# A two-layer graph attention kernel: an overflow test without bounds, the query by one VectorE operation, more buffers, and another order of setup and end

## The chip, the core and the metric

The kernel runs on one core of a Trainium2 chip. The time is device microseconds of one launch, the median of several runs. All runs quoted of one kernel, taken together, agree within about 0.3%. The profile is one further execution, recorded with the hardware profiler.

## The reference, cut to what matters

32 images of 512 nodes by 512 features, float32, one 512 x 512 adjacency matrix of zeros and ones for all. Two layers, each on a normalised input and added to it:

```python
# layer 0: attention of 8 heads, 64 wide
h = relu(layernorm(x))
q, k, v = h @ Wq + bq, h @ Wk + bk, h @ Wv + bv          # split into heads
s = q @ k.T / sqrt(64) + (1 - adj) * -1e9
x = x + (softmax(s) @ v) @ Wo + bo
# layer 1: graph attention
h = relu(layernorm(x))
g = h @ W;  s1 = g @ a1;  s2 = g @ a2
e = leaky_relu(s1[i] + s2[j], 0.2) * adj
x = x + elu(softmax(e) @ g + beta * g)
```

The kernel takes the softmaxes without subtracting a row maximum. That is right as long as no exponential overflows, so it has to find out at the end whether one could have; if so, a slow general path does everything again. With these inputs that path never runs.

## The kernel before: the parts concerned

The work is a software pipeline. In one iteration TensorE does the scores and the attention of image b, the projections of image b+1, the output projection and the logits of layer 1 of image b-1, and the final stage of layer 1 of image b-2. TensorE's order is written by hand; that of the other engines is made by the framework from the program and from when it thinks an operand is ready.

The query leaves PSUM through ScalarE and is scaled on GpSimd. Both projections are read a second time for a bound on the scores:

```python
def proj_q(b, hT, f, qT):                       # [...] the matmuls into p
    qf = wtile([P, N], f"qf_{b}_{f}", "qf", 1)
    nc.scalar.activation(qf, p, AF.Identity, bias=bq_c[:, f : f + 1])
    q = wtile([P, N], f"qT_{b}_{f}", "qT", 6)
    nc.gpsimd.tensor_tensor(q, qf, edge8, op=ALU.mult)
    bound(b, f, qm[:, f, :], p, bq_c[:, f : f + 1])

def bound(b, f, m, p, bias):                    # [...] first image of a group of 8
    r = wtile([P, N], f"ab_{b}_{f}", "ab", 1, BF16)
    nc.scalar.activation(r, p, AF.Abs, bias=bias)
    nc.vector.tensor_tensor(m, m, r, op=ALU.max)
```

The exponentials `e` of a pair of heads are added up on GpSimd into one buffer `es`, which TensorE then multiplies by ones to have the denominators `pd`:

```python
    if k == 1:
        st["es"][j] = wtile([P, 2, N], f"es_{b}_{j}", "es", 1)      # one buffer
    if k:
        one, es = (st["e"][j][0] if k == 1 else st["es"][j]), st["es"][j]
        for s in range(2):
            nc.gpsimd.tensor_tensor(es[:, s, :], one[:, s, :], e[:, s, :], op=ALU.add)
# attend():
        nc.tensor.matmul(pd[...], ones[:, :HD], st["es"][j][:, s, :], start=True, stop=True)
    nc.vector.reciprocal(rd, pd)
    nc.gpsimd.tensor_tensor(o, o, rd, op=ALU.mult)
```

The final stage ends on GpSimd with the addition of the residual `x1`, whose buffer the load of a later residual waits for. That load is followed on GpSimd by an addition of a constant row, and in the same queue stand the small powers that give each row its 1/sqrt(variance):

```python
def final(b, t, st):                            # [...] matmuls into p
    nc.scalar.activation(y, p, AF.Exp, scale=r)
    nc.vector.tensor_scalar(y, y, 1.0, -1.0, op0=ALU.min, op1=ALU.add)      # the clamp
    nc.vector.scalar_tensor_tensor(y, p, r, y, op0=ALU.mult, op1=ALU.max)
    nc.gpsimd.tensor_tensor(y, y, st["x1"][t], op=ALU.add)
    nc.sync.dma_start(out[b, ts(t, P), :], y)
def residual(b, st):                            # for each t
    nc.sync.dma_start(r, x[b, ts(t, P), :])
    nc.gpsimd.tensor_tensor(r, r, c_row, op=ALU.add)
def stats(...):                                 # [...] mean and variance on VectorE
    nc.gpsimd.tensor_tensor(rstd, rstd, mhalf[:, 0:1], op=ALU.pow)
```

## Time and profile before

| | before |
|---|---|
| median of the first 3 runs | 4221.7 us (4221.6 to 4225.3) |
| TensorE busy | 94% |
| setup, until the pipeline's first transposition | 104.2 us |
| pipeline, until the last value projection | 3896.4 us |
| tail | 220.5 us |

The same three stretches, as the trace has them (columns: from:to, us, then busy us of TensorE, its weight loads, VectorE, ScalarE and GpSimd with counts, the granted clock, the DMA share and GB/s):

```profile
0.00:104.20 104.20, 62.04 (x142) 28.84 (x143) 31.91 (x72) 19.64 (x31) 21.30 (x32) 0.93 0.30 101
104.20:4000.60 3896.40, 3754.54 (x11051) 1507.40 (x11049) 2306.43 (x3131) 1344.72 (x1865) 1836.78 (x1553) 0.99 0.08 24
4000.60:4221.10 220.50, 166.96 (x442) 66.68 (x442) 97.78 (x161) 46.66 (x64) 73.09 (x62) 0.87 0.07 23
```

What TensorE waited for before (who waited, for which engine's writing, total us, times, the longest):

```profile
PE ps L268 <- DVE e L272: 51.2, 27, 3.3
PE pk L226 <- DVE at L351: 45.3, 25, 3.9
PE pq L215 <- ACT ab L238: 18.6, 20, 2.3
...
PE pe L367 <- POOL as L361: 17.4, 2, 8.8
PE pbs L116 <- DVE dgs L111: 14.9, 2, 7.6
```

The first three recur in most iterations (20 to 27 of 31) and are the three holes that the prediction shows in one of them. The last two come twice, at the end, and are the holes of the tail. One caution in reading them: in about every other iteration some of TensorE's matmuls ran slowly (from 632 to 641 us the granted clock was 0.81), and its waits were then shorter by what it lost. The iteration that starts at 411.1 us has 5.3 us of waits. In the next one the eight score matmuls take 2.88 us and not 2.26, those of the query projection 4.45 and not 3.70, 1.4 us lost together though the wait before them was only 1.9 us, and the waits come to 3.9 us. Both iterations took 127.82 us.

### The profile page before, as it was taken

What the parts mean: (1) busy time and instruction counts of PE and PEld (TensorE: products, weight loads), DVE (VectorE), ACT (ScalarE), POOL (GpSimd) and SP (SyncE); (2) the same over time, 40 slices, a digit from 0 to 9 for tenths busy, and PEclk for the clock granted to TensorE, in tenths of its full rate; (3) what the DMA queues carried; (4) which work ended last, traced back from release to release, by engine and by line L of the source; (5) the groups of instructions that cost most, each with busy time, mean ns of one, the idle gap of its engine ahead of it and who ended that gap; (6) DMA issues with size and microseconds to landing.
All of it is one profiled execution on the core that took longest, in us unless ns stands there. A gap on an engine that the chain in (4) does not pass through costs nothing.

```text
span 4221.1 us, 32429 instructions
## 1 busy us (share of the span) xinstructions
PE 3983.5 (94%) x11632; PEld 1602.9 (38%) x11632; DVE 2436.1 (58%) x3364; ACT 1411.0 (33%) x1960; POOL 1931.2 (46%) x1647
## 2 busy tenths in 40 slices
PE   5999999999999999999999999999999999999986
PEld 2333333333343333333333333333433333333332
DVE  3556655556655566555666555666555665556663
ACT  1433333333333333333333333333333333333321
POOL 2444544445444445444545444454444454444451
PEclk9999999999999999999999999999999999999988
DMA  2000000000110000100000100001100001000000
GB/s 100 20 10 30 20 30 25 26 20 20 30 30 25 20 25 20 30 28 22 20 30 20 30 25 25 20 21 30 30 25 20 25 20 30 29 21 11 20 20 28
DMA packets 59000, 109.91 MB, mean 26 GB/s; under 512 B 6416, under 2 KB 6416, under 8 KB 58832
## 3 DMA queue, kind: packets, MB, share of 16 engines
q1 hardware_dynamic: 55824, 101.74, 7.9%
q10 hardware_dynamic: 2640, 5.24, 0.4%
q8 instruction: 93, 1.52, 0.2%
q0 software_dynamic: 368, 0.79, 0.1%
q14 instruction: 75, 0.61, 0.0%
HBM read 74.19 MB, written 33.55 MB: 26 GB/s over the span
## 4 chain that ended last, share of the span: by engine, by line
PE 60%; DVE 20%; POOL 7%; ACT 6%; DMA 5%; issue 1%; SPq 0%; ACTq 0%; POOLq 0%; DVEq 0%
PE pg L380 11%; PE pv L258 11%; PE po L290 8%; PE py L390 8%; PE pk L226 6%; PE ps L268 6%; DMA x<-in_x_dram 4%; PE pq L215 4%; DVE e L272 3%; DVE scr L337 3%; PE pw L319 3%; DVE rd L303 2%; POOL rs L184 2%; DVE x L200 2%; ACT e L275 2%; PE pd L297 2%
## 5 line engine op out<-in xcount | busy, mean ns | idle before, releaser
L282 POOL TENSOR_TENSOR es<-es,e 128x512 f32<-128x512 f32 x512 | 671.6, 1340 | 476.2 <-ACT e L275 476.2
L272 DVE TENSOR_TENSOR e<-ps,nmT 128x1024 f32<-128x1024 f32 x512 | 608.0, 1215 | 476.6 <-PE ps L268 476.6
L275 ACT ACTIVATE e<-e 128x1024 f32<-128x1024 f32 x512 | 541.1, 1057 | 747.8 <-DVE e L272 724.6
L282 POOL TENSOR_TENSOR es<-e,e 128x512 f32<-128x512 f32 x256 | 323.8, 1286 | 700.3 <-PE pd L297 696.3
L303 DVE RECIPROCAL rd<-pd 128x512 f32<-128x512 f32 x128 | 429.4, 3355 | 365.2 <-PE pd L297 365.2
L268 PE MATMUL ps<-qT,kT 64*128 64x512 f32 x2048 | 527.3, 631 | 52.6 <-DVE e L272 51.2
L226 PE MATMUL pk<-hT,wk 128*128 128x512 f32 x1024 | 482.7, 616 | 55.7 <-DVE at L351 45.3
L215 PE MATMUL pq<-hT,wq 128*128 128x512 f32 x1024 | 476.9, 609 | 22.0 <-ACT ab L238 18.6
L390 PE MATMUL py<-w,gT 128*128 128x512 f32 x1024 | 472.1, 605 | 0.8 <-ACT ab L238 0.8
L290 PE MATMUL po<-e,v 128*64 128x512 f32 x2048 | 469.9, 601 | 0.0
L319 PE MATMUL pw<-wo,oT 128*128 128x512 f32 x1024 | 463.5, 596 | 4.0 <-DVE y L398 3.6
L380 PE MATMUL pg<-at,hn 128*128 128x512 f32 x1024 | 458.6, 601 | 0.8 <-DVE at L375 0.8
L258 PE MATMUL pv<-wv,hT 128*128 128x512 f32 x1024 | 456.3, 598 | 0.0
L313 POOL TENSOR_TENSOR x<-x,c_row 128x512 f32<-128x512 f32 x128 | 163.0, 1275 | 346.7 <-DMA x<-in_x_dram 346.7
L226 PEld LDWEIGHTS pk<-hT,wk 128*128 128x128 f32 x1024 | 192.1, 194 | 336.7 <-issue 224.4
L268 PEld LDWEIGHTS ps<-qT,kT 64*128 64x128 f32 x2048 | 176.4, 188 | 357.9 <-issue 211.9
L215 PEld LDWEIGHTS pq<-hT,wq 128*128 128x128 f32 x1024 | 193.7, 195 | 299.4 <-issue 218.3
L390 PEld LDWEIGHTS py<-w,gT 128*128 128x128 f32 x1024 | 185.8, 190 | 279.8 <-issue 251.0
L380 PEld LDWEIGHTS pg<-at,hn 128*128 128x128 f32 x1024 | 190.3, 191 | 265.7 <-issue 233.2
L319 PEld LDWEIGHTS pw<-wo,oT 128*128 128x128 f32 x1024 | 194.3, 191 | 253.9 <-issue 242.8
L399 POOL TENSOR_TENSOR y<-y,x 128x512 f32<-128x512 f32 x128 | 162.2, 1267 | 272.7 <-DVE y L398 270.5
L258 PEld LDWEIGHTS pv<-wv,hT 128*128 128x128 f32 x1024 | 189.6, 190 | 243.6 <-issue 215.2
(113 smaller groups left out, 3655.6 us busy)
## 6 DMA issues: line engine op xcount, KB each, us to landing
x<-in_x_dram SPq DMA_DIRECT2D x256, 256.0 KB, 2.9
out_dram<-y SPq DMA_DIRECT2D x128, 256.0 KB, 3.2
wq<-in_L_gnn_Wq_dram ACTq DMA_DIRECT2D x1, 1024.0 KB, 12.7
adj_sb<-in_adj_dram SPq DMA_DIRECT2D x1, 1024.0 KB, 9.6
wk<-in_L_gnn_Wk_dram ACTq DMA_DIRECT2D x1, 1024.0 KB, 16.1
wv<-in_L_gnn_Wv_dram ACTq DMA_DIRECT2D x1, 1024.0 KB, 18.2
wo<-in_L_gnn_Wo_dram ACTq DMA_DIRECT2D x1, 1024.0 KB, 20.4
w<-in_L_gnn_W_dram ACTq DMA_DIRECT2D x1, 1024.0 KB, 17.8
```

The source lines that it names most:

```text
L215: nc.tensor.matmul(p, wq[:, c, ts(f, P)], hT[c], start=c == 0, stop=c == C - 1)
L226: nc.tensor.matmul(p, wk[:, c, ts(f, P)], hT[c], start=c == 0, stop=c == C - 1)
L258: nc.tensor.matmul(p, hT[c][:, ts(t, P)], wv[:, c, :], start=c == 0, stop=c == C - 1)
L268: nc.tensor.matmul(p[:, s, :], st["kT"][j][rows, ts(k, P)], st["qT"][j][rows, :], start=True, stop=True)
L272: nc.vector.tensor_tensor(e, p, nmT[:, k, :].unsqueeze(1).to_broadcast([P, 2, N]), op=ALU.add)
L275: nc.scalar.activation(e, e, AF.Exp)
L282: nc.gpsimd.tensor_tensor(es[:, s, :], one[:, s, :], e[:, s, :], op=ALU.add)
L290: nc.tensor.matmul(po[s * HD : (s + 1) * HD, :], v[k][:, (2 * j + s) * HD : (2 * j + s + 1) * HD], e[k][:, s, :], start=k == 0, stop=k == ...
L303: nc.vector.reciprocal(rd, pd)
L319: nc.tensor.matmul(p, st["oT"][c][:, ts(t, P)], wo[:, c, :], start=c == 0, stop=c == C - 1)
L380: nc.tensor.matmul(p, st["hn"][k][:, ts(c, P)], st["at"][k], start=k == 0, stop=k == T - 1)
L390: nc.tensor.matmul(p, st["gT"][c][:, ts(t, P)], w1[:, c, :], start=c == 0, stop=c == C - 1)
```

## The change

The intent is to take work off the chain between the engines. No bounds are kept: an overflow is found from what it leaves. The values are scaled by 2^60 so that an overflow reaches the means and variances as a value that isn't finite, and the sums of the reciprocals and the totals of layer 1 are checked against 2^60. The query becomes one VectorE operation that reads PSUM. Some buffers become more numerous, the first projections come ahead of the constants, and the end has another order. The core of the diff:

```diff
 def proj_q(b, hT, f, qT):
-        qf = wtile([P, N], f"qf_{b}_{f}", "qf", 1)
-        nc.scalar.activation(qf, p, AF.Identity, bias=bq_c[:, f : f + 1])
         q = wtile([P, N], f"qT_{b}_{f}", "qT", 6)
-        nc.gpsimd.tensor_tensor(q, qf, edge8, op=ALU.mult)
-        bound(b, f, qm[:, f, :], p, bq_c[:, f : f + 1])
+        nc.vector.scalar_tensor_tensor(
+            q, p, bq_c[:, f : f + 1], edge8, op0=ALU.add, op1=ALU.mult
+        )
 def proj_k(b, hT, f, kT):
-        bound(b, f, km[:, f, :], p, bk_c[:, f : f + 1])
 # [...] bound, bound_rows, bound_group removed; in logits():
-        nc.scalar.activation(sa, s12.rearrange("p g t -> p (g t)"), AF.Abs)
-        nc.vector.tensor_tensor(smax, smax, sa, op=ALU.max)
 # [...] value projection: scaled by VS = 2^60; residual: p * 1/VS + x1 in one operation
-            st["es"][j] = wtile([P, 2, N], f"es_{b}_{j}", "es", 1)
+            st["es"][j] = wtile([P, 2, N], f"es_{b}_{j}", "es", 2)
 # [...] likewise rd 1 -> 2, x1 5 -> 6, y 2 -> 3; in attend():
+        nc.scalar.activation(junk, rd, AF.Copy, accum_out=rsum[:, b, j : j + 1])
 # in diagonal():
+        nc.vector.scalar_tensor_tensor(fin, st["mv"], 0.0, fin, op0=ALU.mult, op1=ALU.add)
+        nc.vector.tensor_tensor(dmax[:, 0, :], dmax[:, 0, :], pd[:, :, 0], op=ALU.max)
+        nc.vector.tensor_tensor(dmax[:, 1, :], dmax[:, 1, :], rd, op=ALU.max)
 # the last stages; the verdict (judge) becomes a part of the one before the last
+        if b == B:
+            order = G + Y[:2] + W + Y[2:3] + lg + Y[3:] + D + [judge]
 # setup: first image and Wq first, constants between the projections
+        load_w(wq, Wq)
         new_state(0)
+        load_adj()
+        # [...] the other weights
         norm0(0, states[0]["x"])
         # [...] transpositions
+        edges()
+        first = list(front_groups(0))
+        # first[:4]: the first two query and key projections
+        # [...] load and normalise image 1
+        masks()
+        # first[4:]: the other projections
+        row_constants()
```

More of the change, by code (lines that the diff above doesn't have):

```diff
@@ L23 @@
 BIG = 3.0e38
-LIM0 = 30.0
-LIM1 = 40.0
-GROUP = 8
+VS = 2.0 ** 60
+RMAX = 2.0 ** 60
 def bcast_rows(ap, n):
@@ L72, in ctile, with load_w @@
         return const.tile(shape, dt, name=name, tag=name)
-    def load_w(ap, name):
-        w = ctile([P, C, D], name)
+    wq, wk, wv, wo, w1 = (ctile([P, C, D], n) for n in ("wq", "wk", "wv", "wo", "w1"))
+    def load_w(w, ap):
         nc.scalar.dma_start(w, ap.rearrange("(c p) f -> p c f", p=P))
-        return w
-    wq, wk, wv = load_w(Wq, "wq"), load_w(Wk, "wk"), load_w(Wv, "wv")
-    wo, w1 = load_w(Wo, "wo"), load_w(W, "w1")
     bq_c, bk_c, bv_c = ctile([P, C], "bq_c"), ctile([P, C], "bk_c"), ctile([P, C], "bv_c")
@@ L100 @@
     c_row = ctile([P, D], "c_row")
-    qm, km = ctile([P, C, N], "qm", BF16), ctile([P, C, N], "km", BF16)
-    bmax = ctile([P, N], "bmax")
-    smax = ctile([P, 2 * T], "smax")
+    fin = ctile([P, T, 2], "fin")
+    dmax = ctile([P, 2, T], "dmax")
+    rsum = ctile([P, B, NP], "rsum")
     bad = ctile([P, T], "bad")
-    kv = ctile([P, C, 32], "kv", BF16)
     flag = ctile([1, 1], "flag", I32)
@@ L117, in row_bcast, with wtile, load_adj, edges @@
         return p
-    with tc.tile_pool(name="setup", bufs=1) as work, tc.tile_pool(
-        name="setup_psum", bufs=2, space=bass.MemoryType.PSUM
-    ) as psum:
-        adj_sb = work.tile([P, T, N], F32, name="adj_sb", tag="adj_sb")
-        nc.sync.dma_start(adj_sb, adj.rearrange("(t p) k -> p t k", p=P))
-        deg = work.tile([P, T], F32, name="deg", tag="deg")
-        nc.vector.tensor_reduce(deg, adj_sb, axis=AX.X, op=ALU.max)
-        e0 = work.tile([P, T], F32, name="e0", tag="e0")
-        nc.vector.tensor_scalar(e0, deg, 0.0, 1.0, op0=ALU.is_equal, op1=ALU.mult)
-        sq = work.tile([P, T, N], F32, name="sq", tag="sq")
-        nc.vector.scalar_tensor_tensor(sq, adj_sb, -1.0, adj_sb, op0=ALU.add, op1=ALU.mult)
-        nc.vector.tensor_reduce(bad, sq, axis=AX.X, op=ALU.max, apply_absolute_value=True)
+    nc.vector.memset(fin, 0.0)
+    nc.vector.memset(dmax, 0.0)
+    fast = ExitStack()
+    work = fast.enter_context(tc.tile_pool(name="work", bufs=2))
+    psum = fast.enter_context(tc.tile_pool(name="psum", bufs=2, space=bass.MemoryType.PSUM))
+    def wtile(shape, name, tag, bufs, dt=F32):
+        return work.tile(shape, dt, name=name, tag=tag, bufs=bufs)
+    adj_sb = []
+    def load_adj():
+        for t in range(T):
+            r = wtile([P, N], f"adj_{t}", "at", 4)
+            nc.sync.dma_start(r, adj[ts(t, P), :])
+            adj_sb.append(r)
+    def edges():
+        e0 = wtile([P, T], "e0", "e0", 1)
+        for t in range(T):
+            nc.vector.tensor_reduce(e0[:, t : t + 1], adj_sb[t], axis=AX.X, op=ALU.max)
+        nc.vector.tensor_scalar(e0, e0, 0.0, 1.0, op0=ALU.is_equal, op1=ALU.mult)
         pe0 = row_bcast(psum, work, e0, "e0")
-        e0_r = work.tile([P, N], F32, name="e0_r", tag="e0_r")
-        nc.scalar.copy(e0_r, pe0)
-        nc.vector.tensor_scalar(edge8, e0_r, -(HD ** -0.5), HD ** -0.5, op0=ALU.mult, op1=ALU.add)
+        nc.vector.tensor_scalar(edge8, pe0, -(HD ** -0.5), HD ** -0.5, op0=ALU.mult, op1=ALU.add)
+    def masks():
         for k in range(T):
@@ L140, with row_constants @@
             for t in range(T):
-                nc.tensor.transpose(p[:, ts(t, P)], adj_sb[:, t, ts(k, P)], ident)
+                nc.tensor.transpose(p[:, ts(t, P)], adj_sb[t][:, ts(k, P)], ident)
             nc.scalar.copy(adjT[:, k, :], p)
-            m = work.tile([P, N], F32, name=f"m_{k}", tag="m", bufs=2)
-            nc.vector.tensor_tensor(m, p, e0_r, op=ALU.max)
+            m = wtile([P, N], f"m_{k}", "y", 3)
+            nc.vector.tensor_scalar(m, edge8, -(HD ** 0.5), 1.0, op0=ALU.mult, op1=ALU.add)
+            nc.vector.tensor_tensor(m, p, m, op=ALU.max)
             nc.vector.tensor_scalar(nmT[:, k, :], m, -NEG, NEG, op0=ALU.mult, op1=ALU.add)
-        wa = work.tile([P, 2, C], F32, name="wa", tag="wa")
+        for t in range(T):
+            sq = wtile([P, N], f"sq_{t}", "y", 3)
+            nc.vector.scalar_tensor_tensor(sq, adj_sb[t], -1.0, adj_sb[t], op0=ALU.add, op1=ALU.mult)
+            nc.vector.tensor_reduce(
+                bad[:, t : t + 1], sq, axis=AX.X, op=ALU.max, apply_absolute_value=True
+            )
+    def row_constants():
+        nc.gpsimd.dma_start(c_row, bcast_rows(bo, D))
+        p = psum.tile([P, D], F32, name="pc", tag="mm")
+        for c in range(C):
+            r = wtile([P, P], f"bvr_{c}", "y", 3)
+            nc.vector.tensor_copy(r, bv_c[:, c : c + 1].to_broadcast([P, P]))
+            nc.tensor.matmul(p, r, wo[:, c, :], start=c == 0, stop=c == C - 1)
+        nc.vector.tensor_add(c_row, c_row, p)
+        wa = wtile([P, 2, C], "wa", "wa", 1)
         for g in range(2):
-            ar = work.tile([P, D], F32, name=f"a_{g}", tag="ar", bufs=2)
+            ar = wtile([P, D], f"a_{g}", "x1", 6)
             nc.gpsimd.dma_start(ar, bass.AP(tensor=a.tensor, offset=a.offset + g * D, ap=[[0, P], [1, D]]))
             for c in range(C):
-                scr = work.tile([P, D], F32, name=f"scr_{g}_{c}", tag="scr", bufs=2)
+                scr = wtile([P, D], f"scr_{g}_{c}", "y", 3)
                 nc.vector.tensor_tensor_reduce(
@@ L160 @@
             nc.scalar.copy(dst, p)
-        nc.gpsimd.dma_start(c_row, bcast_rows(bo, D))
-        p = psum.tile([P, D], F32, name="pc", tag="mm")
-        for c in range(C):
-            r = work.tile([P, P], F32, name=f"bvr_{c}", tag="bvr", bufs=2)
-            nc.vector.tensor_copy(r, bv_c[:, c : c + 1].to_broadcast([P, P]))
-            nc.tensor.matmul(p, r, wo[:, c, :], start=c == 0, stop=c == C - 1)
-        nc.vector.tensor_add(c_row, c_row, p)
-        nc.vector.memset(bmax, 0.0)
-        nc.vector.memset(smax, 0.0)
-        nc.vector.memset(kv, 0.0)
-    fast = ExitStack()
-    work = fast.enter_context(tc.tile_pool(name="work", bufs=2))
-    psum = fast.enter_context(tc.tile_pool(name="psum", bufs=2, space=bass.MemoryType.PSUM))
-    def wtile(shape, name, tag, bufs, dt=F32):
-        return work.tile(shape, dt, name=name, tag=tag, bufs=bufs)
     def stats(src, t, u, mv, rstd):
@@ L215, in proj_q @@
             nc.tensor.matmul(p, wq[:, c, ts(f, P)], hT[c], start=c == 0, stop=c == C - 1)
-        qf = wtile([P, N], f"qf_{b}_{f}", "qf", 1)
-        nc.scalar.activation(qf, p, AF.Identity, bias=bq_c[:, f : f + 1])
         q = wtile([P, N], f"qT_{b}_{f}", "qT", 6)
-        nc.gpsimd.tensor_tensor(q, qf, edge8, op=ALU.mult)
-        bound(b, f, qm[:, f, :], p, bq_c[:, f : f + 1])
+        nc.vector.scalar_tensor_tensor(
+            q, p, bq_c[:, f : f + 1], edge8, op0=ALU.add, op1=ALU.mult
+        )
         qT.append(q)
@@ L228, in proj_k @@
         nc.scalar.activation(k, p, AF.Identity, bias=bk_c[:, f : f + 1])
-        bound(b, f, km[:, f, :], p, bk_c[:, f : f + 1])
         kT.append(k)
-    def bound(b, f, m, p, bias):
-        if b % GROUP == 0:
-            nc.scalar.activation(m, p, AF.Abs, bias=bias)
-        else:
-            r = wtile([P, N], f"ab_{b}_{f}", "ab", 1, BF16)
-            nc.scalar.activation(r, p, AF.Abs, bias=bias)
-            nc.vector.tensor_tensor(m, m, r, op=ALU.max)
-    def bound_rows(b):
-        kx = wtile([P, C], f"kx_{b}", "kx", 1)
-        nc.vector.tensor_reduce(kx, km, axis=AX.X, op=ALU.max)
-        nc.vector.tensor_copy(kv[:HD, :, 0:1], kx[:HD].unsqueeze(2))
-        nc.vector.tensor_copy(kv[HD:, :, 1:2], kx[HD:].unsqueeze(2))
-    def bound_group(b):
-        p = psum.tile([P, N], F32, name=f"pbd_{b}", tag="mm")
-        for f in range(C):
-            nc.tensor.matmul(p[ts(f, 32), :], kv[:, f, :], qm[:, f, :], start=True, stop=True)
-        nc.vector.tensor_tensor(bmax, bmax, p, op=ALU.max)
     def proj_v(b, hT, t, v):
@@ L259, in proj_v @@
         s = wtile([P, D], f"v_{b}_{t}", "v", 8)
-        nc.scalar.copy(s, p)
+        nc.scalar.mul(s, p, VS)
         v.append(s)
@@ L301, in attend @@
         nc.scalar.copy(o, po)
-        rd = wtile([P, N], f"rd_{b}_{j}", "rd", 1)
+        rd = wtile([P, N], f"rd_{b}_{j}", "rd", 2)
         nc.vector.reciprocal(rd, pd)
+        junk = wtile([P, N], f"rj_{b}_{j}", "rj", 1)
+        nc.scalar.activation(junk, rd, AF.Copy, accum_out=rsum[:, b, j : j + 1])
         nc.gpsimd.tensor_tensor(o, o, rd, op=ALU.mult)
@@ L310, in residual @@
         for t in range(T):
-            r = wtile([P, D], f"x1_{b}_{t}", "x1", 5)
+            r = wtile([P, D], f"x1_{b}_{t}", "x1", 6)
             nc.sync.dma_start(r, x[b, ts(t, P), :])
@@ L322, in out_proj @@
         x1 = st["x1"][t]
-        nc.vector.tensor_tensor(x1, p, x1, op=ALU.add)
-        mv = wtile([P, 2], f"mv1_{b}_{t}", "mv1", 4)
+        nc.vector.scalar_tensor_tensor(x1, p, 1.0 / VS, x1, op0=ALU.mult, op1=ALU.add)
+        if t == 0:
+            st["mv"] = wtile([P, T, 2], f"mv1_{b}", "mv1", 2)
+        mv = st["mv"][:, t, :]
         rstd = wtile([P, 1], f"rs1_{b}_{t}", "rs1", 4)
@@ L335, in out_proj @@
         for g, r in ((0, wa1_r), (1, wa2_r)):
-            scr = wtile([P, D], f"scr_{b}_{t}_{g}", "y", 2)
+            scr = wtile([P, D], f"scr_{b}_{t}_{g}", "y", 3)
             nc.vector.tensor_tensor_reduce(
@@ L344, in logits @@
         s12 = st["s12"]
-        sa = wtile([P, 2 * T], f"sa_{b}", "sa", 2)
-        nc.scalar.activation(sa, s12.rearrange("p g t -> p (g t)"), AF.Abs)
-        nc.vector.tensor_tensor(smax, smax, sa, op=ALU.max)
         p = row_bcast(psum, work, s12[:, 0, :], f"s1_{b}")
@@ L394, in final @@
         r = st["rd1"][:, t : t + 1]
-        y = wtile([P, D], f"y_{b}_{t}", "y", 2)
+        y = wtile([P, D], f"y_{b}_{t}", "y", 3)
         nc.scalar.activation(y, p, AF.Exp, scale=r)
@@ L438, in dense @@
         D = of(prev, lambda n, i: diagonal(n, s), 1)
-        whole = nxt is not None and (nxt % GROUP == GROUP - 1 or nxt == B - 1)
-        K = [(lambda: bound_rows(nxt)) if whole else None]
-        Q = [(lambda: bound_group(nxt)) if whole else None]
-        order = (
-            G + [Y[0], F[0], Y[1], F[1], W[0], Y[2], W[1], F[2], W[2], Y[3], W[3], F[3], F[4]]
-            + L + [F[5]] + lg + [F[6], F[7]] + K + [V[0], V[1]] + D + Q + [V[2], V[3]]
-        )
+        if b == B:
+            order = G + Y[:2] + W + Y[2:3] + lg + Y[3:] + D + [judge]
+        else:
+            order = (
+                G + [Y[0], F[0], Y[1], F[1], W[0], Y[2], W[1], F[2], W[2], Y[3], W[3], F[3], F[4]]
+                + L + [F[5]] + lg + [F[6], F[7]] + V[:2] + D + V[2:]
+            )
         return [g for g in order if g is not None]
@@ L462, in attention, with judge @@
         return units
+    def judge():
+        ok = wtile([P, T, 6], "ok", "ok", 1)
+        nc.vector.tensor_scalar(ok[:, :, 0:2], fin, 0.0, 1.0, op0=ALU.is_equal, op1=ALU.mult)
+        nc.vector.tensor_scalar(
+            ok[:, :, 2:4], dmax.rearrange("p g t -> p t g"), RMAX, 1.0, op0=ALU.is_le, op1=ALU.mult
+        )
+        nc.vector.tensor_scalar(ok[:, :, 4], bad, 0.0, 1.0, op0=ALU.is_equal, op1=ALU.mult)
+        rm = wtile([P, NP], "rm", "rm", 1)
+        nc.vector.tensor_reduce(rm, rsum.rearrange("p b j -> p j b"), axis=AX.X, op=ALU.max)
+        nc.vector.tensor_scalar(ok[:, :, 5], rm, RMAX, 1.0, op0=ALU.is_le, op1=ALU.mult)
+        okm = wtile([P, 1], "okm", "okm", 1)
+        nc.vector.tensor_reduce(okm, ok, axis=AX.XY, op=ALU.min)
+        p = psum.tile([1, 1], F32, name="pok", tag="mm")
+        nc.tensor.matmul(p, okm, ones[:, 0:1], start=True, stop=True)
+        nc.vector.tensor_scalar(flag, p, P - 0.5, 1.0, op0=ALU.is_lt, op1=ALU.mult)
     with tc.manual_schedule(engines=PE_ONLY):
+        load_w(wq, Wq)
         new_state(0)
+        load_adj()
+        for w, ap in ((wk, Wk), (wv, Wv), (wo, Wo), (w1, W)):
+            load_w(w, ap)
         norm0(0, states[0]["x"])
@@ L468 @@
             turn(0, states[0]["x"], states[0]["hT"], c)
+        edges()
+        first = list(front_groups(0))
+        for g in first[:4]:
+            g()
         if B > 1:
@@ L471 @@
             norm0(1, states[1]["x"])
-        for g in front_groups(0):
+        masks()
+        for g in first[4:]:
             g()
+        row_constants()
         for b in range(B + 2):
@@ L490 @@
     fast.close()
-    with tc.tile_pool(name="judge", bufs=1) as work, tc.tile_pool(
-        name="judge_psum", bufs=1, space=bass.MemoryType.PSUM
-    ) as psum:
-        m = work.tile([P, 4], F32, name="m", tag="m")
-        nc.vector.tensor_reduce(m[:, 0:1], bmax, axis=AX.X, op=ALU.max)
-        nc.vector.tensor_reduce(
-            m[:, 1:3], smax.rearrange("p (g t) -> p g t", g=2), axis=AX.X, op=ALU.max
-        )
-        nc.vector.tensor_reduce(m[:, 3:4], bad, axis=AX.X, op=ALU.max)
-        mT = psum.tile([4, P], F32, name="mT", tag="mT")
-        nc.tensor.transpose(mT, m, ident)
-        r = work.tile([4, 1], F32, name="r", tag="r")
-        nc.vector.tensor_reduce(r, mT, axis=AX.X, op=ALU.max)
-        rT = psum.tile([1, 4], F32, name="rT", tag="rT")
-        nc.tensor.transpose(rT, r, ident[:4, :4])
-        q = work.tile([1, 4], F32, name="q", tag="q")
-        nc.vector.tensor_copy(q, rT)
-        nc.vector.tensor_scalar(q[:, 0:1], q[:, 0:1], LIM0 / HD ** -0.5, 1.0, op0=ALU.is_gt, op1=ALU.mult)
-        nc.vector.tensor_add(q[:, 1:2], q[:, 1:2], q[:, 2:3])
-        nc.vector.tensor_scalar(q[:, 1:2], q[:, 1:2], LIM1, 1.0, op0=ALU.is_gt, op1=ALU.mult)
-        nc.vector.tensor_scalar(q[:, 3:4], q[:, 3:4], 0.0, 1.0, op0=ALU.is_gt, op1=ALU.mult)
-        nc.vector.tensor_add(q[:, 0:1], q[:, 0:1], q[:, 1:2])
-        nc.vector.tensor_add(q[:, 0:1], q[:, 0:1], q[:, 3:4])
-        nc.vector.tensor_copy(flag, q[:, 0:1])
-    again = nc.values_load(flag[0:1, 0:1], min_val=0, max_val=3,
-                           skip_runtime_bounds_check_because="a sum of three comparisons")
+    again = nc.values_load(flag[0:1, 0:1], min_val=0, max_val=1,
+                           skip_runtime_bounds_check_because="a comparison")
     with tc.If(again > 0):
```

## The prediction

> **What bounds the kernel now.** I read in this order: the busy table, the chain that ended last, a table by stage, one iteration in order of time, and the groups of the operations that the diff touches.
>
> ```profile
> PE 3983.5 (94%) x11632; PEld 1602.9 (38%) x11632; DVE 2436.1 (58%) x3364; ACT 1411.0 (33%) x1960; POOL 1931.2 (46%) x1647
> ...
> PE 60%; DVE 20%; POOL 7%; ACT 6%; DMA 5%; issue 1%; SPq 0%; ACTq 0%; POOLq 0%; DVEq 0%
> ```
>
> TensorE is busy 94% of the span, so everything that can be won lies in its 237 us without work and in the time it ran at half clock. Yet the chain lies on TensorE for only 60%: in part of each iteration it runs through VectorE, GpSimd, ScalarE and a DMA. By stage (columns: us, busy us of PE, PEld, DVE, ACT, POOL with counts, granted clock, DMA share, GB/s):
>
> ```profile
> 0.00:52.40 52.40, 14.88 (x30) 6.92 (x30) 23.01 (x50) 5.38 (x8) 6.04 (x17) 0.98 0.49 165
> 52.40:104.20 51.80, 47.16 (x112) 21.92 (x113) 8.89 (x23) 14.26 (x23) 15.26 (x16) 0.88 0.11 37
> 283.10:3870.80 3587.70, 3457.66 (x10150) 1390.26 (x10149) 2124.14 (x2900) 1229.16 (x1708) 1684.35 (x1429) 0.99 0.08 25
> ...
> 4101.50:4176.70 75.20, 54.35 (x127) 22.70 (x126) 29.20 (x65) 11.60 (x18) 15.98 (x15) 0.84 0.08 25
> 4176.70:4221.10 44.40, 30.34 (x66) 13.05 (x66) 7.55 (x23) 5.09 (x8) 5.05 (x4) 0.85 0.07 25
> ```
>
> Row 1 is the setup: TensorE does 15 us of work in 52. Row 3 is 28 iterations of 128.1 us each, with (3587.7 - 3457.7)/28 = 4.6 us idle each; the clock of 0.99 costs about another 1 us. So an iteration could be at best some 122.5 us. Rows 4 and 5 are the tail, with 21 and 14 us idle.
>
> Where the 4.6 us are lost, in an ordinary iteration (start, length, engine, line, operation; in brackets the idle time before it and who ended it):
>
> ```profile
> 1525.96 1.26 POOL L219 TENSOR_TENSOR qT<-qf,edge 128x512 f32<-128x512 f32 x1
> 1526.04 1.48 DVE L200 TENSOR_SCALAR x<-x,mv,rs 128x512 f32<-128x512 f32 x1 [0.66 <-POOL rs L184]
> ...
> 1529.03 2.26 PE L268 MATMUL ps<-qT,kT 64*128 64x512 f32 x8 [1.97 <-DVE e L272]
> 1530.03 0.73 DVE L351 SCALAR_TENSOR_TENSOR at<-pbs,s,adjT 128x512 f32<-128x512 f32 x1
> ...
> 1531.67 0.68 ACT L238 ACTIVATE ab<-pk,bk_c 128x512 bf16<-128x512 f32 x1
> 1532.39 0.60 DVE L239 TENSOR_TENSOR km<-km,ab 128x512 bf16<-128x512 bf16 x1 [1.62 <-ACT ab L238]
> 1532.40 3.70 PE L215 MATMUL pq<-hT,wq 128*128 128x512 f32 x8 [1.11 <-ACT ab L238]
> ...
> 1537.89 3.70 PE L226 MATMUL pk<-hT,wk 128*128 128x512 f32 x8 [1.79 <-DVE at L351]
> ```
>
> Three TensorE waits (1.97, 1.11 and 1.79 us), all around the logits of layer 1. The second is directly the score bound (ScalarE's second read of the key projection). The third is a PSUM buffer that the four logit operations free late, because VectorE stood 1.62 us waiting for that same bound and then did it. The chain of this iteration leaves TensorE at 1487.8 and returns at 1537.9: for 50 us it is a dependency chain over the small engines.
>
> **What the Trainium skill says.** "TensorE: Matmul & The Clock Gate", Part 1: the clock halves after an idle window of about 3.4 us and comes back after a busy one. The trace agrees: after a wait of 3.25 us at 3970 us the eight matmuls of one projection take 6.65 us, where they take 3.60 elsewhere; so long waits cost about double, and short ones are often free of this. "SBUF — State Buffer", Who interferes with whom: GpSimd shares a port pair with VectorE, and a VectorE operation in a two-port mode or with two SBUF inputs waits for it. The trace agrees: the normalisation above takes 1.48 us beside the q product on GpSimd, and 0.546 in the median. "PSUM — Partial Sum Buffer", The four PSUM rules, states that GpSimd cannot read PSUM; that fits the old route of q, ScalarE to SBUF and then GpSimd. "Perfetto Trace Analysis", Identifying Performance Opportunities: a bubble that repeats can mean too few buffers; here it is the two-buffer PSUM tag of the projections.
>
> **The change part by part.** Groups concerned:
>
> ```profile
> L219 POOL TENSOR_TENSOR qT<-qf,edge 128x512 f32<-128x512 f32 x128 | 166.1, 1297 | 37.5 <-ACT qf L217 37.5
> L239 DVE TENSOR_TENSOR qm<-qm,ab 128x512 bf16<-128x512 bf16 x112 | 87.1, 778 | 121.1 <-ACT ab L238 121.1
> L239 DVE TENSOR_TENSOR km<-km,ab 128x512 bf16<-128x512 bf16 x112 | 57.4, 513 | 143.9 <-ACT ab L238 143.9
> L398 DVE SCALAR_TENSOR_TENSOR y<-py,rd,y 128x512 f32<-128x512 f32 x128 | 96.1, 751 | 4.5
> ```
>
> Engine totals first. ScalarE loses q's eviction (86 us), the absolute values (152 + 22) and the small one of the logits (7), and gains 128 sums of the reciprocals, like the 630 ns exponential of L355, perhaps 0.75 with its accumulator: +96. Net about -170. GpSimd loses 166. VectorE loses 145 for the maxima and 18 for the rest of the bounds; it gains q as one operation on PSUM and one SBUF input, which the L398 row prices at 0.75 us (x128 = +96), the scale in the residual add (0.75 for 0.69, +8), and three small operations per image (about +16). Net -43. TensorE loses 1.6 us. So in totals almost nothing is taken off the bounding engine; the gain must come from waits.
>
> Setup, on the path. The first projection starts at 61.4 us. In the new order the x tiles and Wq are first in their queues: Wq landed 12.7 us after its issue even as it was, the x tiles will land some 4 to 9 us in, and from the issue of x to the first projection took 15.3 us (46.1 to 61.4), of which about 4 were GpSimd stuck on residual adds. With the edge column (adjacency, four reductions, one broadcast matmul) ahead of it I put the first projection at about 18 us, 43 earlier. TensorE then has to do what it did before: transposes of the mask (2 us, plus about 3 of waits on their evictions), row constants (two broadcasts and the bias product, 5.5 us, plus about 2 of waits). 43 - 13 = **30 us**.
>
> Iterations, on the path, following the 50 us chain. (a) At 1530.8 VectorE can go on with the logits at once: the wait of 1.62 and the maximum of 0.60 go, 2.2 us. (b) Just before, the q maximum (0.33) and the port wait of the normalisation (1.48 - 0.55) go, and one q operation of 0.75 comes: 0.5 us. (c) At 1499.4 the chain runs ScalarE q, absolute value, maximum (0.58 + 0.58 + 0.50); one q operation of 0.75 takes their place, about 0.7 us net as the two dot products before it stay. Sum 3.4 of the 5.6 us of idle and slow clock. The chain is not the only limit and the new sums and small maxima take something back; I count 80%, **2.7 us** x 29 iterations = **78 us**.
>
> Buffers: a second row-sum buffer removes GpSimd's waits for the denominators' matmul (696 us, but GpSimd isn't the bound), and a sixth residual buffer starts a load one final stage sooner; twice in the chain GpSimd stands on that load with the rstd behind it. I count both as help for the 80%, not extra.
>
> Tail. In the next-to-last stage TensorE waits 7.32 us for the logits' broadcast and 8.78 for the row sums. Y2 and Y3, 3.43 us each, are moved into these two holes: 7 us. The verdict's serial steps from 4212.0 to 4215.3, behind the last store, go before the last stage: about 4 us with the waits. The wait of 3.60 us for a final stage's buffer may also go: 2. Together **13 us**.
>
> Sum 30 + 78 + 13 = 121; 4221.7 - 121 = about 4100 us, 2.9% faster.
>
> **Rivals.** (1) VectorE takes the place: q's PSUM buffer is now freed by an engine whose queue holds reciprocals of 3.36 us and pairs of score additions of 2.34. With two buffers, an eviction may come one group (3.4 us) late without harm, and VectorE stood idle near three of the four q's; against that, the second and third q fall in the stretch where VectorE is nearly full. If each costs 1 us, the iterations win only 1 us: 4221.7 - 30 - 29 - 13 = 4150. (2) ScalarE stands behind the reciprocal: the new sum waits in its in-order queue for a 3.36 us operation; if that is late, evictions and exponentials behind it are late, and TensorE waits. The gap between the end of the denominators and the next eviction is about one group, so the cost should be tenths; if it is 1 us per head pair, that is 4 per iteration and the gain of the iterations is gone: about 4180. (3) The chain collapses altogether, with the residual loads no longer in it: TensorE is left with 0.4 us per iteration, 5.2 x 29 = 150 won, 4030. (4) Work in totals decides and waits only move: then only setup and tail count, 4180.
>
> **Range and chances.** The setup and tail are nearly certain (35 to 50 us, 1% together), so slower is very unlikely. The line of 2% is 84 us, that is, 41 us from the iterations, 1.4 us each; (a) alone would give that. Predicted 4100, 8 times in 10 between 4055 and 4155; faster by over 2% 0.77, within 2% 0.21, slower 0.02.
>
> **What would show it.** First projection near 18 us and first scores near 76 (now 107). The wait before the second query projection gone, that before the last key projection under 0.6 us, the one before the scores still 1 to 2 us; iterations near 125.4. VectorE near 2390 us, ScalarE 1240, GpSimd 1765. Wrong if TensorE waits for the q operation (rival 1), if ScalarE's idle time is ended by the reciprocal with TensorE behind it (2), or if setup is bound by VectorE or by the weights' landing.

## The result, and the profile after

| | before | after |
|---|---|---|
| median | 4221.66 us (4212.39 to 4225.29, 4 runs) | 4091.32 us (4089.47 to 4092.31, 4 runs) |
| setup | 104.2 us | 92.3 us |
| pipeline | 3896.4 us | 3790.4 us |
| tail | 220.5 us | 206.6 us |

The ratio is 0.9694, with a 95% interval of 0.9677 to 0.9711: 3.1% faster. A ratio here is the mean time of one kernel's fast runs over that of the other's of the same rounds, so it is not quite the ratio of the medians quoted. Of the 131.8 us that the two traces differ, 11.9 lie in the setup, 106.0 in the pipeline (31 iterations, 3.4 us each) and 13.9 in the tail.

The busy table of after, and its chain of work that ended last:

```profile
PE 3950.5 (97%) x11616; PEld 1590.1 (39%) x11616; DVE 2409.2 (59%) x3323; ACT 1254.4 (31%) x1799; POOL 1839.0 (45%) x1519
...
issue 0%; POOL 0%; POOLq 0%
```

The chain is of no use this time: it breaks off at its last instruction. The table by stretch has to take its place (columns as before):

```profile
0.00:92.30 92.30, 57.92 (x143) 26.39 (x144) 40.92 (x89) 11.62 (x18) 19.74 (x29) 0.93 0.34 117
92.30:3882.70 3790.40, 3725.78 (x11035) 1496.88 (x11033) 2271.38 (x3075) 1193.45 (x1709) 1747.00 (x1429) 1.00 0.08 25
3882.70:4089.30 206.60, 166.79 (x443) 66.84 (x442) 96.95 (x159) 49.34 (x72) 72.25 (x61) 0.90 0.07 24
```

Over the pipeline TensorE's time without work falls from 142 to 65 us (3896.4 - 3754.5, and 3790.4 - 3725.8), and the clock is at full speed almost throughout. TensorE's waits after:

```profile
PE pbs L114 <- DVE qT L224: 35.2, 28, 2.6
PE pn L214 <- DVE x L207: 21.8, 1, 21.8
PE pq L222 <- ACT kT L234: 13.9, 26, 0.5
PE pe L350 <- POOL as L344: 12.7, 2, 8.7
PE pbs L114 <- DVE dgs L109: 11.7, 2, 7.6
```

The three recurring waits of before are gone or, before a query projection, down to 0.5 us each. A new one has come in, in 28 of the 31 iterations: the broadcast of the logits (`pbs`) waits for a PSUM buffer that the new query operation on VectorE (line 224) has to free. That is the shape of rival 1. Is the query operation then too slow? These rows of the groups price the new operations (line, engine, operation, out<-in, count, busy us, mean ns, idle before):

```profile
L224 DVE SCALAR_TENSOR_TENSOR qT<-pq,bq_c,edge 128x512 f32<-128x512 f32 x128 | 95.1, 743 | 27.6 <-PE pq L222 27.6
L307 DVE SCALAR_TENSOR_TENSOR x<-pw,x 128x512 f32<-128x512 f32 x128 | 88.0, 688 | 186.7 <-PE pw L303 186.6
...
L359 DVE TENSOR_TENSOR dmax<-dmax,rd 128x4 f32<-128x4 f32 x32 | 33.5, 1048 | 0.0
```

The query takes 743 ns, as estimated; the scaled residual addition takes 688 against 687 before, so the scale costs nothing; only a maximum over 128 x 4 numbers is out of proportion, 1.05 us where its neighbour of the same shape, which reads one input from PSUM, takes 0.13. The trace shows when: in the three executions in which GpSimd is idle it takes 0.16 us; in the other 29 a row-sum addition on GpSimd has begun 0.15 us before it, and it takes 1.14 us, until that addition of 1.25 us is through.

The setup, first on TensorE (start, us, engine, line, operation, in brackets the idle time before it and who ended it), then three lines of VectorE:

```profile
21.84 4.50 PE L214 MATMUL pn<-ident,x 128*128 128x128 f32 x16 [21.84 <-DVE x L207]
26.18 2.08 PE L114 MATMUL pbe<-dge,ones 128*128 128x512 f32 x2
28.04 2.21 PE L222 MATMUL pq<-hT,wq 128*128 128x512 f32 x4
...
87.60 2.04 PE L114 MATMUL pbwa<-dgwa,ones 128*128 128x512 f32 x2 [10.05 <-DVE dgwa L109]
```

```profile
19.64 0.69 DVE L140 TENSOR_REDUCE e<-adj 128x1 f32<-128x512 f32 x1 [0.75 <-DMA adj<-in_adj_dram]
...
21.25 1.91 DVE L207 TENSOR_SCALAR x<-x,mv,rs 128x512 f32<-128x512 f32 x4
...
75.01 0.23 DVE L169 COPY bvr<-bv_c 128x128 f32<-128x128 f32 x1 [17.27 <-PE pc L170]
```

The first projection starts at 28.0 us, not at 18: VectorE has the four reductions of the adjacency in its queue ahead of the four normalisations, and the last adjacency tile is there only at 19.6 us. The DMA engines are fully busy by then (the view gives a share of 1.05 from 12 to 20 us), with the weights too; that these delay the adjacency is likely, but no run took them away. Then 10 us go at the end of the setup, behind a VectorE copy that waits 17.3 us for TensorE to free a buffer.

### The profile page after: what moved, and what is told of

The parts are those of the page before. It is cut to its first block, busy times and chain, and to the rows that moved or that the text cites. A ratio compares the mean times of both kernels' runs of the same rounds, so it can differ in the third digit from the quotient of the medians.

```text
span 4089.3 us, 32221 instructions
## 1 busy us (share of the span) xinstructions
PE 3950.5 (97%) x11616; PEld 1590.1 (39%) x11616; DVE 2409.2 (59%) x3323; ACT 1254.4 (31%) x1799; POOL 1839.0 (45%) x1519
## 5 line engine op out<-in xcount | busy, mean ns | idle before, releaser
L264 POOL TENSOR_TENSOR es<-es,e 128x512 f32<-128x512 f32 x512 | 713.2, 1423 | 460.7 <-ACT e L257 460.7
L222 PE MATMUL pq<-hT,wq 128*128 128x512 f32 x1024 | 467.8, 600 | 14.6 <-ACT kT L234 13.9
L264 POOL TENSOR_TENSOR es<-e,e 128x512 f32<-128x512 f32 x256 | 343.8, 1363 | 282.5 <-ACT e L257 282.5
L232 PE MATMUL pk<-hT,wk 128*128 128x512 f32 x1024 | 467.2, 599 | 0.8 <-DVE at L334 0.8
L288 POOL TENSOR_TENSOR oT<-oT,rd 128x512 f32<-128x512 f32 x128 | 171.3, 1338 | 625.2 <-DVE rd L285 544.8
L323 DVE CUSTOM_DVE_ANT_0 scr<-hn,wa_r 128x512 f32<-128x512 f32 x256 | 267.8, 1083 | 68.9 <-ACT hn L317 68.9
## 6 DMA issues: line engine op xcount, KB each, us to landing
adj<-in_adj_dram SPq DMA_DIRECT2D x4, 256.0 KB, 11.9
```

The lines of the kernel that those rows point to most:

```text
L222: nc.tensor.matmul(p, wq[:, c, ts(f, P)], hT[c], start=c == 0, stop=c == C - 1)
L232: nc.tensor.matmul(p, wk[:, c, ts(f, P)], hT[c], start=c == 0, stop=c == C - 1)
```

## The experiments

Twelve kernels ran. All but the last two give the reference's result. The expectations name the accounts of the gain by letters: A is that of the prediction, in which the bounds carry what is won in an iteration; B gives it to the added buffers; C to GpSimd's query products, which hold up VectorE through the shared port; under B and C alike the bounds alone bring almost nothing.

### The kernel before without the bounds alone

```diff
-        bound(b, f, qm[:, f, :], p, bq_c[:, f : f + 1])
-        bound(b, f, km[:, f, :], p, bk_c[:, f : f + 1])
-        sa = wtile([P, 2 * T], f"sa_{b}", "sa", 2)
-        nc.scalar.activation(sa, s12.rearrange("p g t -> p (g t)"), AF.Abs)
-        nc.vector.tensor_tensor(smax, smax, sa, op=ALU.max)
-        whole = nxt is not None and (nxt % GROUP == GROUP - 1 or nxt == B - 1)
+        whole = False
```

> The kernel before with the score bounds alone taken out (absolute values, maxima, group bounds; q still by ScalarE and GpSimd, old buffers, old setup and end). Theory A (the prediction: the second read of the key projection by ScalarE and the maximum behind it hold the logits and with them TensorE): 2 to 2.5 us less per iteration, about 4221 - 70 = 4150 us, and the wait of the last key projection's matmuls under 0.6 us. Theory B (buffers: GpSimd standing on the denominators and on the residual loads sets the 50 us chain): within 25 us of the kernel before, about 4205. Theory C (GpSimd's q products, by the shared port): the same as B here, about 4205.

Measured: 4086.55 us (4085.56 to 4087.43), ratio 0.9692 (0.9676 to 0.9708). This is as fast as the whole change, and nearly twice what account A had. Its waits:

```profile
PE ps L263 <- DVE e L267: 18.5, 31, 2.2
...
PE pq L212 <- ACT kT L224: 15.0, 28, 0.5
...
PE pk L222 <- DVE at L343: 0.8, 1, 0.8
```

The 51.2, 18.6 and 45.3 us of before have become 18.5, 15.0 and 0.8. (No run takes ScalarE's second reads and VectorE's maxima away separately, so how the gain divides between them stays open.) In its trace the pipeline takes 3763.9 us, 132.5 less than before or 4.3 per iteration. Therefore everything else in the change, taken together, has to give nothing, although setup and tail are shorter by 26 us. Something in it costs.

### The query by one VectorE operation, on top of that

```diff
-        qf = wtile([P, N], f"qf_{b}_{f}", "qf", 1)
-        nc.scalar.activation(qf, p, AF.Identity, bias=bq_c[:, f : f + 1])
-        nc.gpsimd.tensor_tensor(q, qf, edge8, op=ALU.mult)
+        nc.vector.scalar_tensor_tensor(
+            q, p, bq_c[:, f : f + 1], edge8, op0=ALU.add, op1=ALU.mult
+        )
```

> As e1, and q by one VectorE operation. Theory A: some 20 us less than e1, about 4130 (0.5 to 0.7 us per iteration). Theory C: 70 us or more less than e1, GpSimd's share of the contention on the normalisation gone, its mean from 0.80 to 0.55 us. Rival 1 of the prediction (VectorE frees q's buffer late): e2 slower than e1 by 10 us or more.

Measured: 4076.88 us (4074.11 to 4081.38), ratio 0.967 (0.9654 to 0.9686), 10 us less than without it. So the query operation isn't what costs, and rival 1 falls. VectorE takes over 95 us of work and gets 28 back in one place, the normalisation of the next image; first the kernel without the bounds alone, then this one:

```profile
L197 DVE TENSOR_SCALAR x<-x,mv,rs 128x512 f32<-128x512 f32 x128 | 100.7, 786 | 36.7 <-POOL rs L181 36.3
```

```profile
L197 DVE TENSOR_SCALAR x<-x,mv,rs 128x512 f32<-128x512 f32 x128 | 72.3, 565 | 36.2 <-POOL rs L181 35.6
```

786 ns become 565 with the product on GpSimd gone that ran beside it. That much of account C came true, but not its 70 us.

### The new buffers, on top of that

```diff
-# [...] buffers of the tags: "es", 1   "rd", 1   "x1", 5   "y", 2
+# [...] buffers of the tags: "es", 2   "rd", 2   "x1", 6   "y", 3
```

> As e2, with the new numbers of buffers (row sums 2, reciprocals 2, residual 6, results 3); setup and end still the old ones, no sums of reciprocals. If the setup gave 12 us and the end 14, as the stretches of the two traces say, the iterations gave about 106, so this should stand at 4115. Theory A: within 15 us of e2. Theory B: 40 us or more under e2.

Measured: 4113.05 us (4110.63 to 4116.05), ratio 0.9757 (0.974 to 0.9773). The buffers do not help, they cost 36 us. Account B has the wrong sign.

### The changed kernel with the old order of the setup

```diff
         load_w(wq, Wq)
-        new_state(0)
         load_adj()
         # [...] the other weights
+        edges()
+        masks()
+        row_constants()
+        new_state(0)
         # [...] and none of the three later on
```

> The changed kernel with all constants ahead of the first image again (adjacency, masks, row constants, then x and the projections). The two traces put what the setup gave at 12 us: 4091 + 12 = 4103. The prediction's 30 us would make it 4121. If the order of the setup is worth nothing by itself: 4091.

Measured: 4100.07 us (4098.35 to 4101.23), ratio 0.9723 (0.9706 to 0.9739). The new order is worth 8.8 us, not 30. In this trace the setup takes 101.0 us.

### The changed kernel with one row-sum buffer

```diff
-            st["es"][j] = wtile([P, 2, N], f"es_{b}_{j}", "es", 2)
+            st["es"][j] = wtile([P, 2, N], f"es_{b}_{j}", "es", 1)
```

> The changed kernel with one row-sum buffer again instead of two. New theory D (from e2 against e3): with one buffer GpSimd's first addition of a head pair waits for the same matmuls as VectorE's reciprocal, which reads PSUM, and so runs beside it at no cost; with two it runs earlier, beside VectorE operations on SBUF, and holds them up. D expects 30 to 40 us less than the changed kernel, about 4057, the dot products' mean back from 1083 to about 940 ns and TensorE's wait for the q operation from 1.2 to under 0.4 us per iteration. If one of the other buffers is what costs (residual, results, reciprocals): 4091, unchanged.

Measured: 4055.45 us (4052.81 to 4056.05), ratio 0.9613 (0.9599 to 0.9626): 36 us faster than the changed kernel. The wait of TensorE for the query operation is all but gone; in the changed kernel it was 35.2 us in 28 times:

```profile
PE pbs L114 <- DVE qT L224: 3.0, 4, 1.2
```

The other sign that theory D named did not come: the dot products take 1080 ns in the mean, against 1083, and not 940. So the time is as D said, and its mechanism is already in doubt here.

### The changed kernel without the sums of the reciprocals

```diff
-        nc.scalar.activation(junk, rd, AF.Copy, accum_out=rsum[:, b, j : j + 1])
```

> The changed kernel without ScalarE's sums of the reciprocals (the overflow test is then incomplete; the outputs are the same). Rival 2 of the prediction (ScalarE stands behind the reciprocal): 20 us or more less. Otherwise within 8 us of 4091, as e3, which has none, has the same iterations of 124.7 us.

Measured: 4094.31 us (4091.33 to 4095.18), ratio 0.9703 (0.969 to 0.9716). Taking the 128 sums off ScalarE wins nothing, so rival 2 falls too.

### The changed kernel with the old end

```diff
-        if b == B:
-            order = G + Y[:2] + W + Y[2:3] + lg + Y[3:] + D + [judge]
-        else:
+        if True:
             # the order of every iteration; judge() after the last stage
```

> The changed kernel with the old order of the last image's groups, and the verdict after the last stage. The tails of the two traces say that the new order gave 14 us, the prediction 13: about 4104. If the waits in the tail only move: 4091 to 4095 (the verdict alone).

Measured: 4095.93 us (4095.26 to 4096.69), ratio 0.9709 (0.9695 to 0.9722): the new end is worth 4.6 us by the medians, not the 13 expected; the tail in the trace is 213.8 us against 206.6. The wait of the row sums there is back at 17.4 us, 12.7 with the new end:

```profile
PE pe L350 <- POOL as L344: 17.4, 2, 8.8
```

### The changed kernel with other buffers for the bias rows

```diff
-            r = wtile([P, P], f"bvr_{c}", "y", 3)
+            r = wtile([P, P], f"bvr_{c}", "at", 4)
```

> The changed kernel with the four bias columns of the setup in buffers of another tag than the dot products' results. In the trace TensorE waits 10.05 us at the end of the setup for these dot products, which stand behind the fourth bias column, which waits for a buffer that the bias product frees only after the projections. If that is the cause of most of the shortfall of the setup, 8 to 10 us less, about 4082; if GpSimd's residual additions beside them are: under 4 us.

Measured: 4081.15 us (4079.09 to 4081.57), ratio 0.9672 (0.9659 to 0.9685): 10 us faster, as expected. With a buffer for each of the four bias rows VectorE doesn't stand behind TensorE and has the row constants ready in time. The wait of 10.05 us is 1.8:

```profile
PE pbwa L114 <- DVE dgwa L109: 1.8, 1, 1.8
```

### A version meant to beat both

It takes the changed kernel with one row-sum buffer and the other bias-row buffers, puts the loads of the first image ahead of Wq and on two queues, and uses the new group order in the iteration before the last stages too:

```diff
-            nc.sync.dma_start(r, x[b, ts(t, P), :])
+            (nc.scalar if b == 0 and t >= T // 2 else nc.sync).dma_start(r, x[b, ts(t, P), :])
-        if b == B:
-            order = G + Y[:2] + W + Y[2:3] + lg + Y[3:] + D + [judge]
+        if b >= B - 1:
+            order = G + Y[:2] + W + Y[2:3] + lg + Y[3:] + D + [judge] * (b == B)
-        load_w(wq, Wq)
         new_state(0)
+        load_w(wq, Wq)
```

> A version to beat both: the changed kernel with one row-sum buffer (e5, 36 us), the bias columns in another tag (e8, 10 us), the first image's x tiles issued from both queues ahead of Wq (the first projection at 28 us stands on x tiles that land up to 14 us in; 3 to 6 us), and the new order of the groups for the last but one loop too, where TensorE waits 7.6 and 8.7 us for the logits (4 to 8 us). Sum: 4091 - 56 = about 4035 us; 4045 if the last two give nothing.

Measured: 4030.69 us (4030.02 to 4033.74), ratio 0.9565 (0.9552 to 0.9578), 4.3% faster than before and 60.6 us faster than the change. Some 46 us of this are the two parts tested above; the new loads and the new group order were not run apart. TensorE is busy 98%:

```profile
PE 3937.3 (98%) x11616; PEld 1585.1 (39%) x11616; DVE 2405.2 (60%) x3323; ACT 1256.6 (31%) x1799; POOL 1809.5 (45%) x1519
```

### The second row-sum buffer by itself

The kernel of the second experiment with `"es", 2` in place of `"es", 1` and nothing else.

> e2 (no bounds, q by VectorE, all else old, 4077 us) with two row-sum buffers and nothing else. Theory D: all of the 36 us that e3 stands over e2 come from this buffer, so 4110 to 4115, the dot products at 1.1 us against 0.94, and TensorE waiting about 1 us per iteration for the q operation. If the residual or result buffers do it: 4077.

Measured: 4115.67 us (4111.35 to 4117.53), ratio 0.9763 (0.975 to 0.9777), 38.8 us slower than with one buffer. So this one number does it; the other new buffers, in the third experiment, add nothing that these runs can tell. The wait of TensorE for the query operation, with one buffer and then with two:

```profile
PE pbs L114 <- DVE qT L214: 3.6, 7, 1.0
```

```profile
PE pbs L114 <- DVE qT L214: 32.6, 28, 2.4
```

The sign expected on the dot products of layer 1 did not come here either: their mean is 938 ns, 936 with one buffer. What did change is the clamp of the final stage, in the mean from 652 to 945 ns. The same place of the same iteration, on GpSimd, with one buffer (the iteration with two lies 12.21 us later, so take that from its times):

```profile
1456.56 1.31 POOL L299 TENSOR_TENSOR oT<-oT,rd 128x512 f32<-128x512 f32 x1 [2.91 <-ACT oT L296]
1459.64 1.27 POOL L391 TENSOR_TENSOR y<-y,x 128x512 f32<-128x512 f32 x1 [1.76 <-DVE y L390]
1464.67 1.26 POOL L308 TENSOR_TENSOR x<-x,c_row 128x512 f32<-128x512 f32 x1 [3.76 <-DMA x<-in_x_dram]
...
1467.80 2.49 POOL L277 TENSOR_TENSOR es<-e,e 128x512 f32<-128x512 f32 x2
```

With two buffers:

```profile
1468.78 1.31 POOL L299 TENSOR_TENSOR oT<-oT,rd 128x512 f32<-128x512 f32 x1 [2.91 <-ACT oT L296]
1470.05 3.13 POOL L277 TENSOR_TENSOR es<-e,e 128x512 f32<-128x512 f32 x2
1473.14 1.28 POOL L391 TENSOR_TENSOR y<-y,x 128x512 f32<-128x512 f32 x1
1477.53 1.26 POOL L308 TENSOR_TENSOR x<-x,c_row 128x512 f32<-128x512 f32 x1 [3.12 <-DMA x<-in_x_dram]
```

The pair of first additions of the next row sum has moved ahead of the final stage's last addition, since it no longer has to wait for the denominators' matmul. The last addition starts 1.29 us later (1473.14 - 12.21 - 1459.64), the residual that is loaded after it lands later, its addition starts 0.65 us later (1477.53 - 12.21 - 1464.67), and everything behind it in the queue too. At the end of that chain TensorE waits 1.00 us for the query operation where it waited 0.35.

Two things could make the last addition late. The pair stands ahead of it in the queue; and the pair runs beside the clamp, which takes 1.48 us here and 0.41 with one buffer (first one buffer, then two):

```profile
1458.36 0.41 DVE L389 TENSOR_SCALAR y<-y 128x512 f32<-128x512 f32 x1
```

```profile
1470.57 1.48 DVE L389 TENSOR_SCALAR y<-y 128x512 f32<-128x512 f32 x1
```

The 37.6 us by which the 128 clamps together grow (83.4 to 121.0 us) are just about the 39 us that the kernel loses. That is a tempting number. The last two runs test it.

### Both again, without the clamp

One line is taken out of each of the last pair, so the result is wrong, and only its time counts:

```diff
-        nc.vector.tensor_scalar(y, y, 1.0, -1.0, op0=ALU.min, op1=ALU.add)
```

With one row-sum buffer:

> e2 (no bounds, q by one VectorE operation, one row-sum buffer) with the final stage's clamp on VectorE taken out; the result is wrong on purpose. It is the base line for e12. With one buffer the clamp is short (0.41 us at the place that counts), so all theories say little is won: 0 to 0.4 us per iteration, 4065 to 4077 us.

With two:

> e10 (the same with a second row-sum buffer, 39 us slower than e2) with the same clamp taken out; wrong on purpose. Two theories of what the second buffer costs. Port theory: GpSimd's first row-sum additions now run beside the clamp and stretch it from 0.41 to 1.48 us; without a clamp there is nothing to stretch, so e12 is within 10 us of e11. Queue theory: what counts is that the additions (2.5 us) now stand in GpSimd's queue ahead of the final stage's last addition, whose store frees the way for the residual load; then the loss stays without the clamp, 20 to 39 us over e11. The trace would show the wait for the q operation ahead of the logits' broadcast: about 3 us in all under the first, 20 to 33 under the second.

Measured: 4063.66 us (4063.01 to 4066.42) with one buffer, 4102.88 us (4100.95 to 4106.63) with two; ratios 0.9644 (0.9631 to 0.9657) and 0.9737 (0.9723 to 0.975). The second buffer costs 39.2 us with no clamp there to be stretched. Nor was other work of VectorE stretched in the clamp's place: it is busy 2306.7 us with one buffer and 2302.7 with two. So the port theory falls and the queue theory stands: the agreement of 37.6 with 39 us was chance. GpSimd at the same place, one buffer, then two (12.76 us later):

```profile
1454.67 1.27 POOL L390 TENSOR_TENSOR y<-y,x 128x512 f32<-128x512 f32 x1 [1.30 <-DVE y L389]
1459.69 1.27 POOL L308 TENSOR_TENSOR x<-x,c_row 128x512 f32<-128x512 f32 x1 [3.75 <-DMA x<-in_x_dram]
```

```profile
1466.09 2.94 POOL L277 TENSOR_TENSOR es<-e,e 128x512 f32<-128x512 f32 x2
1469.00 1.26 POOL L390 TENSOR_TENSOR y<-y,x 128x512 f32<-128x512 f32 x1
1473.43 1.27 POOL L308 TENSOR_TENSOR x<-x,c_row 128x512 f32<-128x512 f32 x1 [3.17 <-DMA x<-in_x_dram]
```

With two buffers VectorE has finished `y` at 1467.35, yet the last addition starts only when the pair ends, 1.57 us later than with one buffer; the residual's addition starts 0.98 us later, and in the iteration compared TensorE reaches the logits' broadcast 0.97 us later, with all of its matmuls before that in place to within 0.05 us. The waits of TensorE for the query operation add up to 26.3 us:

```profile
PE pbs L114 <- DVE qT L214: 26.3, 28, 1.7
```

The order of the instructions says the same, in the programs as built and in the traces. With one and with two buffers it is the same on TensorE, VectorE and ScalarE. On GpSimd alone it differs, at two places in each iteration, each time by such a move of a pair. This is the second (+ with two buffers, - with one):

```
 L299 TensorTensor oT_0_1409<-oT_0_1409,rd_0_1411 128x512
+L277 TensorTensor es_2_1502<-e_2_0_1493,e_2_1_1499 128x512 x2
 L391 TensorTensor y_3_1510<-y_3_1510,x_0_3_767 128x512
 L308 TensorTensor x_2_0_1786<-x_2_0_1786,c_row 128x512
 [...]
 L181 TensorTensor rs_4_1_1585<-rs_4_1_1585,mhalf 128x1
-L277 TensorTensor es_2_1502<-e_2_0_1493,e_2_1_1499 128x512 x2
```

At the first place a last addition also comes later, but the power that follows it does not (1444.84 us with two buffers, 1432.62 with one, so 12.22 apart).

The Trainium skill's page "PSUM — Partial Sum Buffer", section "Engine vs sequencer instructions", says that GpSimd's queue is strictly first in, first out. The trace agrees: `y<-y,x` starts at 1469.00, when the pair that began at 1466.09 is through. What no run shows is a kernel with two buffers and GpSimd's old order; that would be the last link.

## Why the prediction was right, and where its sum was not

The predicted 4100 us was met with 4091, inside the range. The direction, the bound and the kind of gain (waits, not totals) were right. The terms were less so: the setup gave 18 us less and the iterations 28 us more than predicted, so that the sum came out within 11 us is partly luck:

| term | predicted | traces |
|---|---|---|
| setup | 30 us | 11.9 us |
| iterations | 78 us (2.7 x 29) | 106.0 us (3.4 x 31) |
| tail | 13 us | 13.9 us |
| sum | 121 us | 131.8 us |

**Setup.** The step "I put the first projection at about 18 us" failed: it was 28.0, which is 33.4 us earlier than before and not 43. The load times were taken from before; in the new order the last of the four x tiles is there at 14.0 us, where the prediction had them at 4 to 9, the adjacency at 19.6, and the normalisations stand behind it in VectorE's queue. A second loss was not seen at all: the waits for the row constants, put at 2 us, came to 10.8 at the end, which buffers of another tag take away. The first scores came at 95.3 us, not at 76.

**Iterations.** Of (a) to (c), what belongs to the bounds alone is 1.62 + 0.60 + 0.33 + 0.58 + 0.50 = 3.6 us, which the step "I count 80%" lowers to 2.9. The bounds alone gave 4.3. The discount had the wrong sign: a further piece of the bounds on the same chain was left out, the maximum for another key block (0.34, at 1522.7 us), and the row of before prices the query's maximum at 0.78 us in the mean where the iteration shown happened to have 0.33. The query gave 0.3, where the terms as priced come to about nothing (0.93 + 0.58 - 0.75 - 0.75); the step is right in that the stretch of the normalisation pays for the new operation. Of the signs that the prediction named, the wait before the scores was to stay at 1 to 2 us and has gone too (3.2 us in all); an ordinary iteration takes 124.9 us (3495.8 us for 28), where 125.4 was predicted.

**Buffers.** The step that failed in kind is "I count both as help". The second row-sum buffer did remove GpSimd's waits for the denominators, as said, 696 us of them. It cost 1.1 us per iteration by the traces, since those waits had kept work that nobody was waiting for behind work on the chain. The account of an iteration is then 4.3 + 0.3 - 1.1 = 3.5, for 3.4 measured.

**Tail.** The size was right, but not for the reason given. By the traces the new order accounts for 7.2 of the 13.9 us (213.8 - 206.6), and by the medians it is worth 4.6. The removal of the bounds shortened the tail by 5.3 us without any new order (220.5 to 215.2), which the prediction did not have; the two make up nearly all of it.

**Rivals.** Rival 1 predicted a wait of TensorE for the query operation, and just this wait appeared, 35.2 us of it, yet the query was only the last link; with one row-sum buffer the same operation causes 3.0 us. Rival 2 did not happen. Rival 3 nearly did, in the kernel with one row-sum buffer: its pipeline takes 3755.4 us, 141 less than before, of the 150 that a collapse of the chain was to bring. Rival 4 is refuted by the 106 us of the iterations.

**Engine totals.** VectorE was put near 2390 us and took 2409.2, ScalarE near 1240 and took 1254.4. GpSimd was put near 1765 and took 1839.0; 62 us of the difference are its row-sum additions, which became longer (995 us before, 1057 after). These totals say little of the time, which hangs on what part of this work lies on the chain.

## What to carry to other kernels

A wait that a buffer causes can be a free piece of scheduling: before adding a buffer on an engine with a first-in-first-out queue, ask which work will now stand ahead of which, and whether the work behind it is on the chain that TensorE waits for. The operation named by a wait is the last link, not the cause; follow it back, and take the suspected cause away before you believe a sum that happens to fit. And test a change of several parts one part at a time: here one part gave all that the whole gave, and another part, the second row-sum buffer, took away somewhat more (36 us) than the rest had added (31 us).

## What the Trainium skill lacked or had wrong

- "Perfetto Trace Analysis", section "Identifying Performance Opportunities", says that a repeating bubble can mean too few buffers. It lacks the reverse: a second buffer for the row sums made a repeating bubble, 32.6 us in all where there were 3.6, and cost 38.8 us, by changing the order of GpSimd's queue.
- "SBUF — State Buffer", section "Who interferes with whom", is borne out for the direction (the clamp takes 0.41 us alone and 1.48 us beside GpSimd's additions). It lacks the warning that such a conflict, though seen in the trace, need not cost the kernel anything: with the clamp taken out the loss from the second buffer stayed, 39.2 us.
